# First-group weight sums read from a PSUM bank, and three weight blocks summed one group later

## The chip, the cores and the metric

The kernel runs on one core of a Trainium2 chip. The metric is the device time of one execution in microseconds (us); less is better. PE is the matrix engine, PEld its weight loads, DVE the vector engine, ACT the scalar engine, POOL is GpSimd, SP the engine whose queue issues all DMAs here. One group is 1024 of the 4096 tokens.

## What is computed

Cut to what matters, with `xn` the layer-normalised input (4096 tokens x 1024):

```python
g = sigmoid(xn @ gate_w.T + gate_b)          # the gate: first 1024 tokens feed the mean and y
h = silu(silu(xn @ w1.T) @ w3.T) @ w2.T      # experts' common network
out[top2 expert index] += gate * h           # so only rows 0..7 of the sum are not zero
x = x + s * silu(out)                        # s: recurrence over the gated, normalised input
```

Only rows 0 to 7 of the flattened output differ from the input; the kernel copies the rest. All products are float32. The mean over each batch row of the gated input needs the gate on the first 1024 tokens alone, so the gate product (kind `g`) exists for group 0 only; the two network products (kinds `u` for `w1` and `m` for `w3`) are made for all four groups.

## The kernel before, in words

**Products.** Each 1024 x 1024 x 1024 product is split once into 2 x 2 blocks of 512 and made with seven block products instead of eight (Strassen's scheme in Winograd's form). The seven are numbered 1 to 7. Each needs a left operand (a block of tokens, or one of the sums s1 to s4, lines 680 to 723) and a right operand (a block of a weight, or one of the sums T5, T6, T7, T4, made by `five`, `six`, `seven`, `four`, lines 557 to 584, for `w1` and `gate_w`, and by `take`, line 626, for `w3`). The change's title calls the sums of `six` and `four` T2 and T4. Each such block is a tile `b` of [128, 4, 512], so one sum is four instructions of 128x512.

**Inner level.** A block product that is not "plain" is split a second time in the same way (class `Half`, lines 762 to 846): seven small products of eight matmuls each, with four inner left sums (`left_sums`, 725) and four inner right sums (`fresh_sums`, 487, by `t_sum`, 471), all of them on POOL into tiles `q` of [128, 512]. A plain block product has eight small products and needs no inner sums. Plain are `u` 1 of group 0, `g` 1 and 2, and `m` 2 and 7 of group 0 (`PLAIN_M`).

**Results.** A small product lies in a PSUM tile X, Z or Y (X and Z have two buffers, Y one). Its result is taken out by ACT if it is the first of its output (`first`, 781), otherwise by DVE with an add `b<-X,b` ("drain" below). `whole` (879) adds finished blocks on DVE, and `done` starts the SILU on ACT.

**Later groups.** Groups 1 to 3 don't make the right operands again: `keep_block` and `keep_quarter` (475 to 485) write sums of group 0 to DRAM, `load_kept` and `load_kept_sum` (513, 519) read them. Three blocks have no inner sums from group 0, because they are plain there: `w1` block 1, whose four sums are made early in group 0 beside the product, by `kept_sums_1` (540), only to be kept; and `w3` blocks 2 and 7, whose sums are made in group 1 by `fresh_sums` with kind `m` and sb = 1 (lines 1097 to 1103), used there and kept for groups 2 and 3.

**Order.** The order of all instructions is written out by hand. A clock of "places" runs from 0 to 446 or so; each small product stands at one place (line 1151), other work is put at a place by `at(place, f)`, and a generator's `yield n` puts its rest n places later. Every engine executes its instructions in the resulting order, and so does SP its DMAs. `start[kind, group, i]` is the place of block product i: in group 0, `u` 2 at 16, 5 at 31, 6 at 45, 7 at 59, 4 at 73 and 3 at 87, with `g` three places after each and interleaved; then `m` 1, 5, 6, 2, 7, 4, 3 at 101, 108, 115, 122, 130, 138, 145; then seven places for each block product: `u` of group 1 from 152, `m` of group 1 from 201, with `m` 2 at 222 and `m` 7 at 229; `u` of group 2 from 250.

```python
def s_engine(kind, sb):
    return pool if kind == "u" and sb > 0 else dve
...
at(S(5) - 13, five)
at(S(6) - 16, six)
at(S(7) - 12, seven)
at(S(4) - 14, four)
```

So `five` (POOL) stands at places 18 and 21, `six` (DVE) at 29 and 32, `seven` (POOL) at 47 and 50, `four` (POOL) at 59 and 62, each first for `u` and then for `g`. s1 and s2 of `u` in group 0 are on DVE at 24 and 25, s4 at 75.

**Memory.** There are 20 tiles `b` and 18 tiles `q`, handed out first in, first out. `acc` is a PSUM bank that holds the scattered result from the middle of group 0's last stage on; before, it serves once for a row of statistics. `ps_acc` has a second tag, "rows", for the normalisation's rows of each group (`norm`, 352: DMA to a `q`, ACT copies it to the bank `bc`, DVE reads it from there).

Of the kernel before, what the change touches and what calls it, by code (L numbers as in the profile page):

```python
# [10 lines left out]
F32 = mybir.dt.float32  # L11
# [3 lines left out]
ALU = mybir.AluOpType  # L15
AX = mybir.AxisListType
P = 128
# [5 lines left out]
def kernel(  # L23
# [50 lines left out]
    H = 512  # L74
# [4 lines left out]
    class Pinned:  # L79
# [16 lines left out]
    pe, dve, act, pool, sync = (  # L96
        Pinned(e) for e in (nc.tensor, nc.vector, nc.scalar, nc.gpsimd, nc.sync)
    )
# [9 lines left out]
    ps_acc = ctx.enter_context(tc.tile_pool(name="ps_acc", bufs=1, space=bass.MemoryType.PSUM))  # L108
# [25 lines left out]
    def block(uses=1):  # L134
        return Held(blocks, uses)

    def quarter(uses=1):
        return Held(quarters, uses)
# [34 lines left out]
    acc = ps_acc.tile([P, H], F32, tag="acc", name="acc")  # L173
# [5 lines left out]
    def at(place, f, *args):  # L179

        seq[0] += 1
        heapq.heappush(todo, (place, seq[0], f, args))
# [17 lines left out]
    PLAIN_M = (2, 7)  # L200
# [7 lines left out]
    start = {}  # L208
# [244 lines left out]
    raw = {1: (0, 0), 2: (1, 0), 3: (1, 1)}  # L453
    weights = {"w1": w1, "gw": gw, "w3": w3}
    kept = {}
    op_t = {}
    op_ts = {}

    T_OF = ((1, 0, None), (3, None, 0), (3, 1, None), (2, None, 1))
    T_AT = (1, 2, 4, 6)  # L460
# [10 lines left out]
    def t_sum(o, t, s, j):  # L471
        p, q, e = T_OF[j]
        pool.tensor_tensor(o.tile, t[:, p], t[:, q] if q is not None else s[e].tile, ALU.subtract)

    def keep_quarter(name, i, j, o):
        d = dramp.tile([P, 2 * Q], F32, tag=f"{name}_{i}_{j}", name=f"{name}_{i}_{j}")
        sync.dma_start(d, o.tile)
        kept[name, i, j] = d
        o.drop()
# [4 lines left out]
        kept[name, i] = d  # L484
        t.drop()

    def fresh_sums(kind, sb, i, t, keep):

        name = {"u": "w1", "g": "gw", "m": "w3"}[kind]
        s = []  # L490
        for j in range(4):

            o = quarter(1 + (j < 2) + keep)
            t_sum(o, t, s, j)
            s.append(o)
            if j in (1, 3):
                s[(j - 1) // 2 if j == 1 else 1].drop()
            op_ts[kind, sb, i, j] = o
            if keep:
                at(start[kind, sb, i] + 2 * T_AT[j], keep_quarter, name, i, j, o)  # L500
            if j < 3:
                yield (T_AT[j + 1] - T_AT[j]) * 2
        t.drop()

    def sub(eng, out, p, q, n=4):

        for h in range(0, 4, 4 // n):
            eng.tensor_tensor(
                out[:, h : h + 4 // n], p[:, h : h + 4 // n], q[:, h : h + 4 // n], ALU.subtract
            )  # L510
            yield 0.5

    def load_kept(kind, sb, i, fresh):
        name = {"u": "w1", "m": "w3"}[kind]
        t = block(1 + fresh)
        sync.dma_start(t.tile, weights[name][raw[i]] if i in raw else kept[name, i])
        op_t[kind, sb, i] = t

# [5 lines left out]
    def first_weights(kind, name, before=()):  # L524

        keep = name == "w1"

        def S(i):
            return start[kind, 0, i]

        b = {}

        def load(key, KN, uses, *before):
            b[key] = load_w(name, KN, uses, *before)

        def one():

            op_t[kind, 0, 1] = b[1]

        def kept_sums_1():  # L540
            s = []
            for j in range(4):
                o = quarter(1 + (j < 2))
                t_sum(o, b[1], s, j)
                s.append(o)
                if j == 1:
                    s[0].drop()
                if j == 3:
                    s[1].drop()
                at(S(1) + 18 + 3 * j, keep_quarter, name, 1, j, o)  # L550
                yield 3
            b[1].drop()

        def two():
            op_t[kind, 0, 2] = b[2]

        def five():
            yield from sub(pool, b[5], b[5], b[1])
            b[1].drop()
            op_t[kind, 0, 5] = b[5]  # L560
            if keep:
                keep_block(name, 5, b[5])

        def six():
            yield from sub(dve, b[6], b[6], b[5])
            b[5].drop()
            op_t[kind, 0, 6] = b[6]
            if keep:
                keep_block(name, 6, b[6])

        def seven():

            yield from sub(pool, b[7], b[6], b[7])
            b[6].drop()
            op_t[kind, 0, 7] = b[7]
            if keep:
                keep_block(name, 7, b[7])

        def four():
            yield from sub(pool, b[4], b[4], b[6])  # L580
            b[6].drop()
            op_t[kind, 0, 4] = b[4]
            if keep:
                keep_block(name, 4, b[4])

        def three():
            op_t[kind, 0, 3] = b[3]

        off = 0 if kind == "u" else 1
        load(1, (0, 0), 2 + keep, before)  # L590
        one()
        if keep:
            at(S(1) + 8, kept_sums_1)
        at(-20 + off, lambda: load(2, (1, 0), 2))
        at(-19, two)
        at(-12 + off, lambda: load(5, (0, 1), 3 + keep))
        at(S(5) - 13, five)
        at(2 + off, lambda: load(6, (1, 1), 4 + keep))
        at(S(6) - 16, six)
        at(S(6) - 3 + off, lambda: load(7, (0, 0), 2 + keep))  # L600
        at(S(7) - 12, seven)
        at(S(6) + 8 + off, lambda: load(4, (1, 0), 2 + keep))
        at(S(4) - 14, four)
        at(S(3) - 14, lambda: load(3, (1, 1), 2))
        at(S(3) - 13, three)
        for i in order["u"][1:]:
            if kind == "g" and i in PLAIN_G:
                at(S(i) - 4, lambda i=i: op_t[kind, 0, i].drop())
                continue
            at(  # L610
                S(i) + 2 - (11 if i == 2 else 6),
                lambda i=i: fresh_sums(kind, 0, i, op_t[kind, 0, i], keep),
            )

    def first_w3():


        def S(i):
            return start["m", 0, i]

        b = {}

        def load(key, KN, uses):
            b[key] = load_w("w3", KN, uses)

        def take(i, p=None, q=None):

            if p is not None:
                for h in range(4):
                    dve.tensor_tensor(b[i][:, h], b[p][:, h], b[q][:, h], ALU.subtract)  # L630
                    yield 1
                (b[p] if i == q else b[q]).drop()
                keep_block("w3", i, b[i])
            op_t["m", 0, i] = b[i]

        for place, i, KN, uses in (
            (S(1) - 28, 1, (0, 0), 3),
            (S(1) - 27, 5, (0, 1), 4),
            (S(1) - 20, 6, (1, 1), 5),
            (S(2) - 14, 2, (1, 0), 2),  # L640
            (S(2) - 8, 7, (0, 0), 3),
            (S(7) - 10, 4, (1, 0), 3),
            (S(3) - 14, 3, (1, 1), 2),
        ):
            at(place, load, i, KN, uses)
        at(S(1) - 22, take, 1)
        at(S(1) - 20, take, 5, 5, 1)
        at(S(1) - 12, take, 6, 6, 5)
        at(S(2) - 8, take, 2)
        at(S(2) - 2, take, 7, 6, 7)  # L650
        at(S(7) - 3, take, 4, 4, 6)
        at(S(3) - 8, take, 3)
        for i in order["m"]:
            if i in PLAIN_M:
                at(S(i) - 4, lambda i=i: op_t["m", 0, i].drop())
                continue
            at(
                S(i) + 2 - {1: 16, 5: 12, 6: 10}.get(i, 6),
                lambda i=i: fresh_sums("m", 0, i, op_t["m", 0, i], True),
            )  # L660


# [426 lines left out]
    for kind, sb, i, plain in line:  # L1089
        h = Half(kind, sb, i, plain)  # L1090
        halves.append(h)
        S = start[kind, sb, i]
        n = 2 if sb == 0 and kind == "u" and i not in PLAIN_G else 1
        if kind != "g" and not plain:
            at(S + 2 - 8, left_sums, kind, sb, i, n)
        if kind != "g" and sb > 0:
            fresh = kind == "m" and sb == 1 and i in PLAIN_M
            at(S - (12 if fresh else 10), load_kept, kind, sb, i, fresh)
            if fresh:
                at(  # L1100
                    S - 5,
                    lambda i=i: fresh_sums("m", 1, i, op_t["m", 1, i], True),
                )
            for j in range(0 if fresh else 4):
                at(S + 2 * T_AT[j] - 9, load_kept_sum, kind, sb, i, j)

    for sb in range(NS):
        n = 2 if sb == 0 else 1
# [26 lines left out]
                )  # L1135
    at(start["u", 1, 1] + 25, recurrence)
    first_w3()

    w2_sb = {}

# [141 lines left out]
```

## Time and profile before

| what | value |
|---|---|
| median of 3 runs | 851.44 us (850.01 to 852.07) |
| the profiled execution | 850.65 us, of which the span from first to last instruction is 848.6 us |
| PE busy | 831.2 us, 98% |
| PEld busy | 701.9 us, 83% |
| DVE busy | 565.7 us, 67% |
| POOL busy | 496.6 us, 59% |
| ACT busy | 234.5 us, 28% |
| granted TensorE clock, mean | 0.997 |
| DMA | 189.71 MB, mean 224 GB/s |

The rows of the profile name a group of like instructions by line, engine, operation and tiles, out<-in. Since every engine call runs through one helper, all of them have line L89, and groups are told apart by tiles: `b` a block, `q` a quarter of one, X_u, Z_u, Y_u the PSUM tiles of kind `u`, `acc` and `bc` the other PSUM banks. In the timeline a row gives the start in us, the length, the engine, the operation, the tiles, how many instructions are merged in it, and in square brackets how long the engine had been idle and what ended that.

### The profile page before, as it was taken

The page shows a single profiled execution, that of the slowest core. Times are in us where ns is not written, and L with a number is a line of the kernel's source. Part 1 is how long each engine was busy: PE and PEld are TensorE (multiplying, and loading weights), DVE is VectorE, ACT ScalarE, POOL GpSimd, SP SyncE. Part 2 cuts the span into 40 slices and gives each one's busy share as a digit, 9 for nine tenths or more (in the row PEclk, how much of TensorE's full clock was granted, in tenths as well). Part 3 has the DMA queues.
Part 4 walks back from the last instruction along what each step waited for, and adds up shares of the span by engine and source line. Part 5 has one row for each costly group of instructions (what it writes and reads, how often), then busy time and mean ns, then how long its engine had stood idle before and what let it go on. Part 6 is the DMA issues. An engine that isn't in the chain of part 4 may idle for free.

```text
span 848.6 us, 11192 instructions
## 1 busy us (share of the span) xinstructions
PE 831.2 (98%) x4103; PEld 701.9 (83%) x4103; DVE 565.7 (67%) x889; ACT 234.5 (28%) x375; POOL 496.6 (59%) x375
## 2 busy tenths in 40 slices
PE   7999999989999999999999999999999999999997
PEld 6886888878888868888888778888888688888882
DVE  6989796988699425575897225775993246546642
ACT  0212213776121207343012226531122021220121
POOL 0389999995628764436866753753449444465400
PEclk9999999999999999999999999999999999999998
DMA  8953447631976877529976757659775455555600
GB/s 335 421 193 131 161 169 273 260 124 51 361 303 216 305 268 255 200 87 343 363 234 242 266 183 267 234 190 398 270 246 183 165 192 209 195 192 191 264 0 2
DMA packets 54013, 189.71 MB, mean 224 GB/s; under 512 B 6140, under 2 KB 9388, under 8 KB 42312
## 3 DMA queue, kind: packets, MB, share of 16 engines
q1 hardware_dynamic: 53960, 189.01, 60.2%
q8 instruction: 33, 0.54, 0.3%
q14 instruction: 20, 0.16, 0.1%
HBM read 165.86 MB, written 39.87 MB: 242 GB/s over the span
## 4 chain that ended last, share of the span: by engine, by line
PE 87%; DVE 7%; DMA 4%; SPq 1%; issue 1%; ACT 0%; DVEq 0%; ACTq 0%
PE X_u L89 21%; PE X_m L89 20%; PE Z_u L89 11%; PE Z_m L89 11%; DVE b L89 7%; PE Y_u L89 5%; PE X_g L89 5%; PE Y_m L89 4%; PE Z_g L89 3%; DMA b<-in_xT 3%; PE acc L89 2%; PE plT L89 2%; DMA b<-in_gw 1%; SPq L89 1%; PE Y_g L89 1%
## 5 line engine op out<-in xcount | busy, mean ns | idle before, releaser
L89 POOL TENSOR_TENSOR q<-b 128x512 f32<-128x512 f32 x144 | 202.8, 1421 | 230.6 <-DVE b L89 51.8
L89 ACT ACTIVATE b<-b 128x512 f32<-128x512 f32 (+1 forms) x152 | 105.0, 695 | 331.2 <-DVE b L89 322.1
L89 DVE TENSOR_TENSOR b<-b,b 128x512 f32<-128x512 f32 x176 | 181.8, 1052 | 3.3 <-POOL q L89 0.5
L89 POOL TENSOR_TENSOR q<-b,q 128x512 f32<-128x512 f32 x91 | 132.1, 1454 | 5.7 <-issue 3.3
L89 POOL TENSOR_TENSOR b<-b,b 128x512 f32<-128x512 f32 x72 | 94.5, 1336 | 40.5 <-PE X_u L89 34.4
L89 DVE TENSOR_TENSOR b<-X_u,b 128x512 f32<-128x512 f32 x87 | 59.9, 689 | 71.4 <-PE X_u L89 70.8
L89 PE MATMUL X_u<-q,q 128*128 128x256 f32 x432 | 103.1, 381 | 0.9 <-DVE b L89 0.9
L89 DVE TENSOR_TENSOR b<-X_m,b 128x512 f32<-128x512 f32 x84 | 57.2, 687 | 62.3 <-PE X_m L89 61.0
L89 PE MATMUL X_m<-q,q 128*128 128x256 f32 x416 | 98.3, 379 | 0.0
L89 PEld LDWEIGHTS X_u<-q,q 128*128 128x128 f32 x432 | 81.1, 190 | 16.1 <-issue 3.0
L89 POOL TENSOR_TENSOR q<-q,b 128x512 f32<-128x512 f32 x53 | 72.5, 1368 | 30.3 <-PE X_u L89 26.2
L89 PEld LDWEIGHTS X_m<-q,q 128*128 128x128 f32 x416 | 79.0, 190 | 10.8
L89 DVE TENSOR_TENSOR b<-b,bc 128x1024 f32<-128x1024 f32 (+1 forms) x62 | 72.8, 1178 | 3.6 <-ACT bc L89 2.5
L89 PE MATMUL X_m<-b,b 128*128 128x256 f32 x272 | 63.7, 380 | 0.9 <-DVE b L89 0.9
L89 PE MATMUL X_u<-b,b 128*128 128x256 f32 x248 | 58.8, 381 | 5.7 <-DVE b L89 5.5
L89 PEld LDWEIGHTS X_m<-b,b 128*128 128x128 f32 x272 | 51.3, 190 | 8.9 <-DVE b L89 1.9
L89 PEld LDWEIGHTS X_u<-b,b 128*128 128x128 f32 x248 | 46.8, 190 | 13.5 <-DVE b L89 6.7
L89 DVE TENSOR_TENSOR b<-Z_u,b 128x512 f32<-128x512 f32 x47 | 32.4, 689 | 28.6 <-PE Z_u L89 28.0
L89 PE MATMUL X_u<-b,q 128*128 128x256 f32 x216 | 51.3, 380 | 0.0
L89 PE MATMUL Y_u<-b,b 128*128 128x256 f32 x216 | 51.3, 380 | 0.0
L89 PE MATMUL Z_u<-q,b 128*128 128x256 f32 x216 | 51.3, 380 | 0.0
L89 DVE TENSOR_TENSOR b<-Z_m,b 128x512 f32<-128x512 f32 x48 | 32.8, 686 | 27.5 <-PE Z_m L89 26.1
(143 smaller groups left out, 1171.5 us busy)
## 6 DMA issues: line engine op xcount, KB each, us to landing
q<-w SPq DMA_DIRECT2D x160, 256.0 KB, 3.3
b<-in_w SPq DMA_DIRECT2D x35, 1024.0 KB, 7.4
b<-w_T SPq DMA_DIRECT2D x24, 1024.0 KB, 5.1
b<-in_xT SPq DMA_DIRECT2D x15, 1024.0 KB, 9.5
w<-q SPq DMA_DIRECT2D x56, 256.0 KB, 5.6
b<-in_x SPq DMA_DIRECT2D x12, 1024.0 KB, 7.3
w_T<-b SPq DMA_DIRECT2D x8, 1024.0 KB, 4.1
b<-in_gw SPq DMA_DIRECT2D x7, 1024.0 KB, 10.2
```

Source lines behind the costliest of these rows:

```text
L89: r = f(*args, **kwargs)
```

## The change

Five edits, of which the first two concern group 0's `u` and `g`:

1. `six` and `four` are made by a new function `with_bank`: ACT copies a quarter of the subtrahend into a PSUM bank (`acc` and a new tile of the tag "rows" by turns), and DVE subtracts with that bank as its second operand. The copy of quarter j+1 is issued ahead of the subtraction of quarter j. `six` was on DVE with both operands in SBUF, `four` on POOL. Places stay.
2. `kept_sums_1` goes. The same four sums of `w1` block 1 are made by `late_sums` from place 115 on (start of `m` 1, plus 14): it reads the block again from DRAM (1 MB), waits 5 places, and makes and keeps one sum every 2.5 places on POOL.
3. `w3` blocks 2 and 7: their inner sums are made by `late_sums` at places 156 and 170, in group 1's `u` stage, each with a load of 1 MB. Group 1's `m` 2 and 7 then take them from DRAM as in groups 2 and 3, so `fresh_sums` for group 1 goes.
4. `take` for `w3` blocks 7 and 4 moves from DVE to POOL, at the same places (120 and 127).
5. `take` for blocks 5 and 6, on DVE, moves two places later (from 81 to 83 and from 89 to 91).

```diff
+    def with_bank(out, p, q):
+        def copy(j):
+            spare[0] += 1
+            ps = acc if spare[0] % 2 else ps_acc.tile([P, H], F32, tag="rows", name="spare")
+            act.copy(ps, q[:, j])
+            return ps
+
+        ps = copy(0)
+        yield 0.5
+        for j in range(4):
+            ahead = copy(j + 1) if j < 3 else None
+            dve.tensor_tensor(out[:, j], p[:, j], ps, ALU.subtract)
+            ps = ahead
             yield 0.5
+    def late_sums(name, i):
+        t = block()
+        sync.dma_start(t.tile, weights[name][raw[i]] if i in raw else kept[name, i])
+        yield 5
+        s = []
+        for j in range(4):
+            o = quarter(1 + (j < 2))
+            t_sum(o, t, s, j)
+            s.append(o)
+            if j in (1, 3):
+                s[j // 2].drop()
+            yield 2.5
+            keep_quarter(name, i, j, o)
+        t.drop()
...
-            yield from sub(dve, b[6], b[6], b[5])
+            yield from with_bank(b[6], b[6], b[5])
...
-            yield from sub(pool, b[4], b[4], b[6])
+            yield from with_bank(b[4], b[4], b[6])
...
-        load(1, (0, 0), 2 + keep, before)
+        load(1, (0, 0), 2, before)
         one()
-        if keep:
-            at(S(1) + 8, kept_sums_1)
...
-                for h in range(4):
-                    dve.tensor_tensor(b[i][:, h], b[p][:, h], b[q][:, h], ALU.subtract)
-                    yield 1
+                yield from sub(pool if i in (7, 4) else dve, b[i], b[p], b[q], 4, 1)
...
-        at(S(1) - 20, take, 5, 5, 1)
-        at(S(1) - 12, take, 6, 6, 5)
+        at(S(1) - 18, take, 5, 5, 1)
+        at(S(1) - 10, take, 6, 6, 5)
...
-            fresh = kind == "m" and sb == 1 and i in PLAIN_M
-            at(S - (12 if fresh else 10), load_kept, kind, sb, i, fresh)
-            if fresh:
-                at(
-                    S - 5,
-                    lambda i=i: fresh_sums("m", 1, i, op_t["m", 1, i], True),
-                )
-            for j in range(0 if fresh else 4):
+            at(S - 10, load_kept, kind, sb, i)
+            for j in range(4):
                 at(S + 2 * T_AT[j] - 9, load_kept_sum, kind, sb, i, j)
...
+    at(start["m", 0, 1] + 14, late_sums, "w1", 1)
+    for n, i in enumerate(PLAIN_M):
+        at(start["u", 1, 1] + 4 + 14 * n, late_sums, "w3", i)
```

## The prediction

> **What bounds the kernel now.** I read the engines' shares first, then PE's waits, then the timeline around each wait.
>
> ```profile
> PE 831.2 (98%) x4103; PEld 701.9 (83%) x4103; DVE 565.7 (67%) x889; ACT 234.5 (28%) x375; POOL 496.6 (59%) x375
> PE X_u L89 <- DVE b L89: 6.4, 4, 2.4
> PE X_m L89 <- DVE b L89: 0.9, 1, 0.9
> ```
>
> PE sets the time. There are 446 small products of eight matmuls, one every 1.73 us where nothing stalls, 770 us in all; the rest is scatter, routing, start and tail, which the change leaves alone. So it can win only PE's waits for DVE, five waits of 7.3 us, and of those one of 1.5 us lies in the first 30 us, ahead of all that is changed. Now the others, each by two starts of PE; a start later than 1.73 us after the one before is lost time.
>
> ```profile
> 50.81 8.61 POOL L89 TENSOR_TENSOR b<-b,b 128x512 f32<-128x512 f32 x7
> 54.63 5.94 DVE L89 TENSOR_TENSOR b<-b,b 128x512 f32<-128x512 f32 x2
> 65.91 1.89 PE L89 MATMUL Z_g<-b,b 128*128 128x256 f32 x8
> 68.66 0.68 DVE L89 TENSOR_TENSOR b<-X_u,b 128x512 f32<-128x512 f32 x1
> 69.39 1.99 PE L89 MATMUL X_u<-b,b 128*128 128x256 f32 x8 [1.59 <-DVE b L89]
> ...
> 158.36 1.16 DVE L89 TENSOR_TENSOR b<-b,b 128x512 f32<-128x512 f32 x1
> 159.12 1.89 PE L89 MATMUL X_g<-q,q 128*128 128x256 f32 x8
> 161.12 0.68 DVE L89 TENSOR_TENSOR b<-X_u,b 128x512 f32<-128x512 f32 x1
> 161.94 1.97 PE L89 MATMUL X_u<-q,q 128*128 128x256 f32 x8 [0.94 <-DVE b L89]
> 170.65 1.89 PE L89 MATMUL Z_g<-q,b 128*128 128x256 f32 x8
> 174.17 0.68 DVE L89 TENSOR_TENSOR b<-X_u,b 128x512 f32<-128x512 f32 x1
> 174.91 1.99 PE L89 MATMUL X_u<-b,b 128*128 128x256 f32 x8 [2.36 <-DVE b L89]
> ```
>
> Each time PE waits for one drain `b<-X_u,b`, which takes 0.68 us itself but stands late in DVE's order behind `b<-b,b`. Stall A (place 31): 3.48 - 1.73 = 1.75. Stall B (places 81 and 87): 2.82 - 1.73 = 1.09, and 4.26 - 1.73 = 2.53, together 3.62. Stall C lies in group 1's `m` stage, at 430.10: 2.81 - 1.73 = 1.08, and 0.17 at 442.46, together 1.25. The sum, 6.6 us, is all there is to win. C has a control in the same profile: busy times by stretch, for group 1 (404 to 432) and the same places of group 2 (584 to 612); columns PE, PEld, DVE, ACT, POOL.
>
> ```profile
> 150.00:176.00 26.00, 22.70 (x104) 19.36 (x104) 25.13 (x32) 20.03 (x27) 26.00 (x17) 1.00 0.58 227
> 404.00:432.00 28.00, 27.08 (x126) 23.52 (x125) 25.16 (x28) 1.10 (x2) 24.39 (x18) 1.00 0.88 333
> 584.00:612.00 28.00, 28.00 (x131) 24.56 (x130) 24.64 (x30) 2.22 (x4) 10.72 (x8) 1.00 0.88 339
> ```
>
> Where POOL is busy 24 to 26 us, PE loses time; where it is busy 10.7, PE loses none, with as much DMA.
>
> **What the Trainium skill says.** "SBUF — State Buffer", Who interferes with whom: a DVE instruction with two SBUF inputs contends with a GpSimd instruction that reads SBUF, and the one that holds the shared pair blocks the other for the whole instruction; with one SBUF input it does not. The trace agrees: `b<-b,b` is 0.69 us alone and 1.16 to 1.75 beside POOL (mean 1052 ns of 176), in the first row above two take 5.94 us until POOL's run ends; the drains with a PSUM operand keep 0.68 beside the same POOL work, and POOL's 1.26 stretches to 1.72 only beside `b<-b,b`. "VectorE: DVE Perf Modes", the errata section: (N+151)/0.96, so 691 ns for 512 elements; the trace has 689 for `b<-X_u,b`. "ScalarE: Activation LUTs", What ACT_TABLE_LOAD costs: an activation without pointer operands is 186 + 0.833 N ns, 613 ns here; the trace has 590 ns for the row copy into a PSUM bank, `bc<-q`, the same operation as the new copies.
>
> **The change part by part.**
>
> Stall A. `kept_sums_1` is four POOL instructions. The first runs in a gap (POOL waits until 38.48 for the normalisation anyway), the other three stand between 39.7 and 48.4 in a run that has no gap until 59.42 and whose end is the seven `b<-b,b` above (`five`). Without them, at 8.61 / 7 = 1.23 us each, POOL's run ends 3.7 us earlier, at 55.7. DVE's first `b<-b,b` of s1 at 54.63 waits for just that, so s1, s2 and the drain behind them come 3.7 us earlier: X_u is free at 65.6 instead of 69.3, and PE wants it at 65.91 + 1.73 = 67.6. Margin 2 us, less up to 1.1 because POOL then also reaches its next sums earlier and contends with s2. Gain 1.75. Four stores of 256 KB leave SP's queue there; nobody waits for them.
>
> `six`: eight DVE `b<-b,b` between 69.26 and 82.8, 12.9 us in all, become eight of 0.69, 5.5 us, and POOL's sums beside them fall towards 1.26. PE has no wait there that this would remove (0 gained), but it covers the new wait: DVE now waits for ACT's copy, and behind the waiting instruction stand drains. Bound: 0 if the copies run ahead, 8 x (0.59 + about 0.1) = 5.5 us if each is waited for. Even then DVE has no more work than before. ACT's copies also stand ahead of its own drains of products 5, so ACT is tied to DVE's lateness; PE gives such a drain four slots, 6.9 us. Cost 0.
>
> `four`: POOL loses eight instructions between 119.5 and 136.5, 8 x about 1.4 = 11 us; DVE gets 8 x 0.69 = 5.5 us at places 59 to 64, 122.9 to 133 us. DVE's work there is six drains (4.1), one `whole` (1.0) and the 5.5, against 6 x 1.73 = 10.4 us of PE: 10.6, just full. The tight spot is the last drain of X_g of product 6 at place 60: PE wants the buffer at 128.03; DVE, free at 125.7, does two subtractions and then the drain, until 127.8. Margin 0.2 us if ACT's copies run ahead, which they can, since their source is ready long before. If not, up to 1 us is lost, and up to 0.6 at place 73 if the lateness isn't made up. Cost 0.4, bounds 0 and 1.6.
>
> Stall B. DVE's s4 stands at places 75 to 76.5: in the timeline four `b<-b,b` of 1.75, 1.16, 1.76 and 1.16, 5.8 us instead of 2.8, then a `whole` of 1.38. After the change POOL is 8 instructions ahead there. It can't use this beyond its next dependency: its left sums for product 3 need s4. So it runs dry some 10 us before s4 is made, s4 runs alone, and DVE leaves place 77 about 3.0 + 0.7 = 3.7 us earlier. That is more than the 1.09 us of B's first stall. After that POOL contends again, as before. The second stall needs the drain at 174.17 to end by about 171.3 (168.93 + 3.45, less the 1.09); it ends at 174.85 - 3.7 = 171.1, and one of the four `take` 5 instructions (1.15) falls behind it because of the shift by two places. But the other three come closer to it. I take 3.0 of 3.62 as won, with bounds 0 and 3.62.
>
> Stall C. The eight POOL sums of `w3` 2 and 7 leave 405 to 431. The stage becomes that of group 2, which has no stall. Gain 1.25. Instead the stage loads 8 x 256 KB more, which group 2 does as well. In group 1's `u` stage (286 to 343) POOL gets eight sums, 8 x 1.27 = 10 us, where it is busy 36 of 57 us and runs some 8 us or more ahead of PE; two loads of 1 MB and eight stores, with SP waiting for POOL at each store, where the DMA share is 0.74. Cost 0, since loads are issued nine places (15 us) ahead of use; at most 0.5.
>
> `take` 7 and 4, and the late sums of `w1`: POOL gets 8 + 4 instructions, 12 x 1.27 to 1.72 = 15 to 21 us, in 226 to 247, where it is idle for 19.7 us; DVE loses 8 x 0.69 = 5.5 us and more. The load of 1 MB at place 115 takes 2.5 us at 413 GB/s in a stretch with DMA share 1.0, and pushes group 1's blocks and rows behind it by as much. The first row copy (ACT, 238.3) waits for its landing already, and DVE's normalisation and drains behind it would be 2 us later; the nearest limit (last drain of `m` 6 before `m` 7 starts at 245.9) leaves about that. Cost 0.2, bounds 0 and 1.
>
> Sum: 1.75 + 3.0 + 1.25 - 0.4 - 0.2 = 5.4 us. From 850.65 that is 845.25. The median of the runs shown is 0.79 above the profiled one; I add half of that, **845.6**.
>
> **Rivals.** Something of 0.3%, 2.55 us, is about what a measurement of this kernel can tell from no change.
>
> First, B stays: POOL isn't dry at s4, or DVE's gated products (`SCALAR_TENSOR_TENSOR`, 1.75 and 1.18 beside POOL) and `take` 5 make up the same lateness. For it: POOL is 100% busy from 150 to 176. Against: the eight removed instructions stand directly ahead. Gain 2.4: 848.6.
>
> Second, the slow side: ACT and DVE go hand in hand at `four`. If each subtraction costs DVE its own 0.69, a copy of 0.59, two hand-overs and its share of the two 1.04 us statistics on ACT at places 60 and 61, about 1.6 us, DVE's work at places 59 to 64 is 4.1 + 1.0 + 12.8 = 17.9 against 10.4, PE waits about 7 us, and B stays. 850.65 - 3.0 + 7.0 + 0.4 = 855.0. It decides from about 1.4 us a subtraction. Against it: two banks, a copy issued ahead, and ACT busy only 10.3 of 36 us from 112 to 148.
>
> Third, no gain: the drains come earlier, but PE meets other late ones at the next places, so the stalls only move. About 851.0. Against it: between the stalls the drains follow their products by about 1.9 us, as early as they can.
>
> **How the numbers follow.** Forecast 0.67, own range 843.6 to 848.0 (all 6.6 won at no cost gives 844.0, or 844.4 with the half added; all costs at their bounds, 1.6 + 0.5 + 1.0, give 848). B stays 0.13, slow side 0.13, no gain 0.07. The range reaches over "B stays", up to 849.3. Faster by over 0.3% means under 848.9: the forecast and over half of the first rival, 0.74. Same 0.13, slower 0.13.
>
> **What would show it.** A: no PE wait at 69, s1's first instruction about 2 us or less instead of 5.3. B: POOL idle some us before s4, the four s4 instructions near 0.69, no PE wait of over 1 us between 155 and 175. C: group 1's `m` stage without a PE wait, POOL near 11 us in 28. `four`: copies `acc<-b` on ACT well ahead of DVE, DVE's `b<-b,acc` rows at 0.69 with no idle time before them. I'm wrong if those rows show DVE idle for ACT, if PE waits for DVE between 125 and 150, or if PE waits for POOL's `q` or for a DMA in groups 0 or 1.

## The result, and the profile after

| | median, us | lowest to highest | runs |
|---|---|---|---|
| before | 851.29 | 849.43 to 852.32 | 8 |
| after | 845.96 | 843.19 to 847.69 | 8 |

The ratio is 0.9936, with a 95% interval of 0.9916 to 0.9956: the change saves 3.7 to 7.2 us. The profiled execution of after took 847.3 us, with a span of 845.5 us and a mean granted clock of 0.993 (before: 850.65, 848.6 and 0.997).

The engines' shares of after, from the page:

```profile
PE 831.8 (98%) x4103; PEld 702.9 (83%) x4103; DVE 555.5 (66%) x889; ACT 243.5 (29%) x391; POOL 489.9 (58%) x375
L89 DVE TENSOR_TENSOR b<-b,b 128x512 f32<-128x512 f32 x160 | 155.4, 988 | 2.8
```

As many instructions on DVE and POOL as before, and 16 more on ACT: the copies. Before, DVE had 176 of `b<-b,b` at a mean of 1052 ns. Now PE's waits for DVE and POOL's `b`:

```profile
PE X_u L89 <- DVE b L89: 2.5, 2, 1.5
PE X_m L89 <- POOL b L89: 0.9, 1, 0.9
```

Of the 7.3 us of before, 3.4 are left. 1.5 of them is the wait ahead of all that was changed. One is what remains of stall B, and the last, for X_m, stands at a place where there was no wait before. I call it stall D. Start of PE by start of PE, with 1.73 us for a product that doesn't stall, the two traces differ in these places and no others by over 0.15 us:

| place | stall, us | before | after |
|---|---|---|---|
| 2 to 3 | head of the program, change only | | +2.1 |
| 31 | A | 1.75 | 0 |
| 81 | B, first | 1.09 | 0 |
| 87 | B, second | 2.53 | 1.15 |
| 130 | D, start of `m` 7 | 0 | 1.02 |
| 229, 236 | C | 1.08 and 0.17 | 0 |

The stalls give 4.46 us. The head takes 2.1 of it back in this execution, because the clock was granted at half for 6.83 us there (last section). Now the rows that answer to those shown of before. The first two fences are timelines of after, around stall A and around stall B.

```profile
46.27 8.65 POOL L89 TENSOR_TENSOR b<-b,b 128x512 f32<-128x512 f32 x7
...
56.68 1.28 DVE L89 TENSOR_TENSOR b<-b,b 128x512 f32<-128x512 f32 x2
...
67.69 0.68 DVE L89 TENSOR_TENSOR b<-X_u,b 128x512 f32<-128x512 f32 x1
67.95 1.89 PE L89 MATMUL Z_g<-b,b 128*128 128x256 f32 x8
69.68 1.89 PE L89 MATMUL X_u<-b,b 128*128 128x256 f32 x8
```

POOL's run of seven ends at 54.92 instead of 59.42. DVE's pair takes 1.28 us instead of 5.94, the drain ends at 68.37, and PE follows on after 1.73 us.

```profile
151.59 1.29 DVE L89 TENSOR_TENSOR b<-b,b 128x512 f32<-128x512 f32 x2
...
153.41 1.28 DVE L89 TENSOR_TENSOR b<-b,b 128x512 f32<-128x512 f32 x2
...
154.22 1.60 POOL L89 TENSOR_TENSOR q<-b 128x512 f32<-128x512 f32 x1 [9.30 <-issue]
...
155.21 1.17 DVE L89 TENSOR_TENSOR b<-b,b 128x512 f32<-128x512 f32 x1
...
161.03 1.89 PE L89 MATMUL X_u<-q,q 128*128 128x256 f32 x8
...
162.96 0.69 DVE L89 TENSOR_TENSOR b<-X_u,b 128x512 f32<-128x512 f32 x1 [1.03 <-PE X_u L89]
...
169.66 1.89 PE L89 MATMUL Z_g<-q,b 128*128 128x256 f32 x8
...
170.14 1.75 DVE L89 TENSOR_TENSOR b<-b,b 128x512 f32<-128x512 f32 x1
...
171.81 0.68 DVE L89 TENSOR_TENSOR b<-X_u,b 128x512 f32<-128x512 f32 x1
...
172.54 1.99 PE L89 MATMUL X_u<-b,b 128*128 128x256 f32 x8 [0.99 <-DVE b L89]
```

The four instructions of s4 are the second of the first row, the two of the row at 153.41, and the one at 155.21 (the first of all is a `whole`). POOL is idle for 9.30 us and starts again at 154.22, just after s4's second instruction is done (154.09). The profile names no releaser, but POOL's next sum reads the two quarters of s4 that these two instructions make. So the first three run at 0.68 us apiece, and the fourth takes 1.17 beside POOL: 3.2 us in place of the 5.8 of before. The first stall of B is gone: PE starts at 161.03 without a wait, and DVE is even idle for 1.03 us ahead of 162.96. Then a `b<-b,b` of 1.75, one of `take` 5, lies straight ahead of the drain that PE waits for at 172.54. Busy times by stretch in after (columns PE, PEld, DVE, ACT, POOL, clock, DMA share, GB/s):

```profile
150.00:176.00 26.00, 25.01 (x116) 21.69 (x115) 22.41 (x32) 21.50 (x31) 21.78 (x15) 1.00 0.51 189
222.00:250.00 28.00, 27.15 (x126) 23.62 (x125) 19.03 (x23) 4.31 (x6) 23.52 (x18) 1.00 1.02 408
404.00:432.00 28.00, 28.00 (x131) 24.56 (x130) 25.00 (x31) 2.22 (x4) 11.28 (x9) 1.00 0.89 341
```

Group 1's `m` stage (404 to 432) has become that of group 2: POOL at 11.28 instead of 24.39, PE at 28.00. The new loss is in the second row. The same stretch in before:

```profile
222.00:250.00 28.00, 28.00 (x131) 24.66 (x130) 23.06 (x32) 4.31 (x6) 7.12 (x6) 1.00 0.89 358
```

There POOL had 7.12 us of work instead of 23.52, and the DMA queues moved 358 GB/s instead of 408.

### The profile page after: what moved, and what is told of

The parts are those of the page before. It is cut to its first block, busy times and chain, and to the rows that moved or that the text cites. A ratio compares the mean times of both kernels' runs of the same rounds, so it can differ in the third digit from the quotient of the medians.

```text
span 845.5 us, 11244 instructions
## 1 busy us (share of the span) xinstructions
PE 831.8 (98%) x4103; PEld 702.9 (83%) x4103; DVE 555.5 (66%) x889; ACT 243.5 (29%) x391; POOL 489.9 (58%) x375
## 4 chain that ended last, share of the span: by engine, by line
PE 92%; DMA 3%; DVE 2%; POOL 1%; issue 1%; SPq 0%; ACT 0%; POOLq 0%; ACTq 0%; DVEq 0%
PE X_u L89 23%; PE X_m L89 20%; PE Z_u L89 12%; PE Z_m L89 11%; PE Y_u L89 6%; PE X_g L89 6%; PE Y_m L89 5%; PE Z_g L89 4%; PE acc L89 2%; PE plT L89 2%; DMA b<-in_w 2%; DMA w<-q 1%; DVE b L89 1%; POOL q L89 1%; PE Y_g L89 1%
## 5 line engine op out<-in xcount | busy, mean ns | idle before, releaser
L89 POOL TENSOR_TENSOR q<-b 128x512 f32<-128x512 f32 x144 | 198.4, 1391 | 232.3 <-DVE b L89 53.6
L89 DVE TENSOR_TENSOR b<-b,b 128x512 f32<-128x512 f32 x160 | 155.4, 988 | 2.8
L89 PE MATMUL X_u<-b,b 128*128 128x256 f32 x248 | 61.5, 394 | 2.8 <-DVE b L89 2.5
L89 PEld LDWEIGHTS X_u<-b,b 128*128 128x128 f32 x248 | 48.9, 198 | 11.0 <-DVE b L89 3.3
L89 PE MATMUL Z_u<-q,q 128*128 128x256 f32 x216 | 51.0, 379 | 0.0
```

The source lines that it names most:

```text
L89: r = f(*args, **kwargs)
```

## Experiments: each edit by itself

Each of these is before with one part of the change put in. What a stall is worth is read from PE's starts, as above, in the one profiled execution of each kernel; the medians are of several runs.

**Edit 1, the bank.** Before, and only:

```diff
-            yield from sub(dve, b[6], b[6], b[5])
+            yield from with_bank(b[6], b[6], b[5])
...
-            yield from sub(pool, b[4], b[4], b[6])
+            yield from with_bank(b[4], b[4], b[6])
```

> The kernel before with edit 1 alone: six and four read their subtrahend from PSUM banks on DVE. Theory (four's eight instructions leave POOL, which then runs dry before s4, so s4 runs alone): the 1.09 us at place 81 goes and the 2.53 us at place 87 falls by about half, since take 5 isn't shifted here; the stalls at 31 (1.75 us) and in group 1's m stage (1.25 us) stay. Gain 2 to 3 us. Rival (what helps at 81 and 87 is the shift of take 5 alone): both stalls stay, gain near zero or a loss, since DVE gets 2.6 us more work in all.

Measured: 846.09 us (845.27 to 846.75, 4 runs), ratio 0.9941 (0.9924 to 0.9958). By its median this edit alone is as fast as the whole change. Stall B loses 3.2 of its 3.62 us (0 and 0.41 are left), more than in after. Stall C stays. Stall A is 0.88 in this execution; the table near the end of the experiments comes back to it.

**Edit 2, the sums of `w1` later.** Before, with `kept_sums_1` and its call taken out, and:

```diff
+    at(start["m", 0, 1] + 14, late_sums, "w1", 1)
```

> The kernel before with edit 2 alone: the four sums of w1 block 1 leave the first products and are made late. Theory (POOL's run of sums ends some 3.7 us earlier, so DVE's s1 starts earlier): the PE stall of 1.75 us at place 31 is gone, those at places 81 and 87 (3.6 us together) and in group 1's m stage (1.25 us) stay; and if the new stall of 1.0 us at the start of m 7 comes from the extra load of 1 MB, it is here as well. Net gain 0.7 to 1.8 us. Rival (the stall at 31 goes because six reads a PSUM bank): it stays here, net gain zero or less. Rival for the new stall (POOL's take 7 and 4): no stall at m 7 here.

Measured: 849.32 us (846.46 to 850.93, 13 runs) against 850.56, ratio 0.9976 (0.9965 to 0.9988). Stall A is gone, B and C stay, and at `m` 7 there is a stall of 0.36 us. POOL's run of seven ends at 54.58 (54.92 in after), and DVE's pair takes 1.28 us. PE is late in this execution, though: its first `g` product starts at 18.96 instead of 16.59.

**Edit 3, the sums of `w3` in group 1's `u` stage.**

```diff
-            fresh = kind == "m" and sb == 1 and i in PLAIN_M
+            fresh = False
...
+    for n, i in enumerate(PLAIN_M):
+        at(start["u", 1, 1] + 4 + 14 * n, late_sums, "w3", i)
```

> The kernel before with edit 3 alone: the sums of w3 blocks 2 and 7 are made in group 1's u stage. Theory: the stalls of 1.08 and 0.17 us in group 1's m stage go, nothing else changes, no new stall from 286 to 345 us. Gain 1.25 us. Rival (the stall there comes from DVE's own load and the DMAs, not from POOL's sums): it stays, and eight more loads of 256 KB make it no better.

Measured: 848.0 us (846.98 to 850.23, 5 runs), ratio 0.9964 (0.9945 to 0.9983). Stall C loses 1.08 + 0.18, nothing comes up in the `u` stage. But stall A is gone here too, without edit 2, and the first stall of B is longer by 0.53 us. Neither can be the work of edit 3, whose first instruction stands at place 156. The last of the experiments come back to stall A.

**Edits 4 and 5, `take`.**

```diff
-                    dve.tensor_tensor(b[i][:, h], b[p][:, h], b[q][:, h], ALU.subtract)
+                    (pool if i in (7, 4) else dve).tensor_tensor(b[i][:, h], b[p][:, h], b[q][:, h], ALU.subtract)
...
-        at(S(1) - 20, take, 5, 5, 1)
-        at(S(1) - 12, take, 6, 6, 5)
+        at(S(1) - 18, take, 5, 5, 1)
+        at(S(1) - 10, take, 6, 6, 5)
```

> The kernel before with edits 4 and 5 alone: take 7 and 4 on POOL, take 5 and 6 two places later. Theory: the stall at place 31 and the one in group 1 stay; of the 3.6 us at places 81 and 87 at most 1 us goes, since one take 5 instruction of about 1.15 us falls behind the late drain; no stall at m 7, because the extra load of 1 MB is missing here. Gain 0 to 1 us. Rival for m 7 (POOL's take 7 and 4 hold PE up, as the profile's releaser says): the stall of about 1 us at m 7 is here.

Measured: 849.7 us (847.85 to 851.39, 13 runs), ratio 0.9991 (0.998 to 1.0002), no change that can be told. No stall at `m` 7. The stall at place 87 falls from 2.53 to 2.07 us. In this execution and in that of edit 2 PE also loses 1.7 us at places 88 and 89, to the clock (last section).

## Experiments: what makes the bank worth its copies

**Both sums on DVE, from SBUF.** After, without the copies:

```diff
-            yield from with_bank(b[6], b[6], b[5])
+            yield from sub(dve, b[6], b[6], b[5])
...
-            yield from with_bank(b[4], b[4], b[6])
+            yield from sub(dve, b[4], b[4], b[6])
```

> The kernel after, with six and four on DVE from SBUF operands, without the bank and the copies: it tells the move off POOL from the bank. Theory (the bank matters, since b<-b,b shares a port with POOL and costs 1.05 to 1.75 us beside it): four's eight subtractions take 8 to 14 us instead of 5.5 at places 59 to 64, where DVE is full already, so PE waits 2 to 6 us for drains between 122 and 150; slower than after by 2 to 6 us. Rival (it is enough that POOL loses the eight instructions): within 1 us of after, no PE wait there.

Measured: 848.99 us (847.71 to 849.92, 18 runs) against 850.74, ratio 0.9978 (0.9969 to 0.9988). Against after, PE loses 2.96 us at place 62, 0.26 at 68 and 0.93 at 73. The timeline of this kernel at place 62:

```profile
126.60 2.82 DVE L89 TENSOR_TENSOR b<-b,b 128x512 f32<-128x512 f32 x2
...
129.35 0.68 DVE L89 TENSOR_TENSOR b<-X_g,b 128x512 f32<-128x512 f32 x1
...
130.08 1.99 PE L89 MATMUL X_g<-b,b 128*128 128x256 f32 x8 [2.79 <-DVE b L89]
```

And of after at the same place:

```profile
126.01 0.67 DVE L89 TENSOR_TENSOR b<-b,acc 128x512 f32<-128x512 f32 x1
126.61 0.67 DVE L89 TENSOR_TENSOR b<-b,spare 128x512 f32<-128x512 f32 x1
...
127.20 0.68 DVE L89 TENSOR_TENSOR b<-X_g,b 128x512 f32<-128x512 f32 x1
...
128.22 1.89 PE L89 MATMUL X_g<-b,b 128*128 128x256 f32 x8
```

The same two subtractions ahead of the same drain take 2.82 us with both inputs in SBUF beside POOL, and 1.27 with one of them in PSUM. At places 31, 81 and 87 this kernel has PE's starts of after, so what is won of stall B is won without the bank, by what POOL no longer has to do. The bank keeps the moved sums from costing PE 4.15 us at places 62 to 73. So it is the bank that makes it pay to have `four` on DVE: without it the kernel keeps only 1.75 us of its gain (850.74 - 848.99) instead of 5.33.

**One bank, no copy ahead.** After, with the ACT copy and the subtraction hand in hand, which is the mechanism of my slow rival:

```diff
-        ps = copy(0)
         yield 0.5
         for j in range(4):
-            ahead = copy(j + 1) if j < 3 else None
-            dve.tensor_tensor(out[:, j], p[:, j], ps, ALU.subtract)
-            ps = ahead
+            act.copy(acc, q[:, j])
+            dve.tensor_tensor(out[:, j], p[:, j], acc, ALU.subtract)
```

> The kernel after, with a single bank (acc) and no copy issued ahead, so that each subtraction waits for its own copy: the slow rival's hand in hand. If it is as that rival priced it, a subtraction costs DVE about 1.4 us (0.69 + 0.59 + two hand-overs) and PE waits 4 to 7 us for drains between 122 and 150. If DVE finds other work between, as its drains stand between the subtractions, PE loses 1 to 3 us. If ACT's copies hide in any case, nothing changes.

Measured: 846.11 us (844.16 to 847.92, 6 runs), ratio 0.994 (0.9922 to 0.9959). PE loses 0.45 us at place 62. The timeline of this kernel there:

```profile
124.52 0.59 ACT L89 COPY acc<-b 128x512 f32<-128x512 f32 x1 [17.99 <-DVE b L89]
...
125.14 0.69 DVE L89 TENSOR_TENSOR b<-b,acc 128x512 f32<-128x512 f32 x1 [0.66 <-ACT acc L89]
...
126.49 1.99 PE L89 MATMUL X_g<-b,b 128*128 128x256 f32 x8 [0.29 <-DVE b L89]
```

The copy takes 0.59 us and DVE waits 0.66 for it, as the rival said, so a subtraction that waits costs about 1.3 us. But the waits don't add up to the 7 us on PE that it foretold. Of the eight subtractions of `four` only four wait, 2.5 us together, for the 0.45 us of PE. Of those of `six` seven wait, 6.0 us together, and PE loses nothing. Which slack takes up the rest, these runs don't show. The second bank saves less than can be told by the medians.

## Experiments: the new stall D, and what is left of B

**The late sums of `w1` later still.** After, and:

```diff
-    at(start["m", 0, 1] + 14, late_sums, "w1", 1)
+    at(start["m", 0, 1] + 26, late_sums, "w1", 1)
```

> The kernel after, with the late sums of w1 block 1 started 12 places (some 21 us) later, so that their 1 MB isn't read among group 1's first loads. Theory (the 1.0 us that PE loses at the start of m 7 comes from DVE waiting for the row copy, whose DMA stands behind that load): it is gone, DVE's wait before its first normalisation falls from 3.1 us to 1 or less; gain about 1 us. Rival (POOL's take 7 and 4 hold PE, as the profile's releaser says): the stall stays.

Measured: 844.68 us (842.81 to 845.23, 4 runs), ratio 0.9917 (0.9892 to 0.9943). Stall D is gone (1.02 less at place 130), nothing else moves.

**`take` 7 and 4 on DVE again.** After, without edit 4:

```diff
-                yield from sub(pool if i in (7, 4) else dve, b[i], b[p], b[q], 4, 1)
+                yield from sub(dve, b[i], b[p], b[q], 4, 1)
```

> After with edit 4 alone undone: take 7 and 4 on DVE. The wait at the start of m 7 stays at about 1.0 us if it is the 1 MB load's doing, as the later load showed. If POOL's additional work also holds it, it falls below 0.7. Otherwise the same as after: 846, at most 0.5 to either side.

Measured: 844.28 us (842.64 to 846.68, 6 runs), ratio 0.9918 (0.9898 to 0.9937). Stall D falls from 1.02 to 0.20. So either step by itself nearly frees the place: D needs both. Three timelines show how. First after:

```profile
226.54 2.84 SPq L89 DMA_DIRECT2D q<-flat  x2
...
238.57 0.59 ACT L89 COPY bc<-q 128x512 f32<-128x512 f32 x1 [9.73 <-POOL b L89]
...
239.19 1.22 DVE L89 TENSOR_TENSOR b<-b,bc 128x1024 f32<-128x1024 f32 x1 [3.10 <-ACT bc L89]
...
241.05 1.69 DVE L89 TENSOR_TENSOR b<-b,b 128x512 f32<-128x512 f32 x1
...
241.82 1.89 PE L89 MATMUL X_m<-b,b 128*128 128x256 f32 x8
...
243.79 0.68 DVE L89 TENSOR_TENSOR b<-X_m,b 128x512 f32<-128x512 f32 x1
244.57 5.42 PE L89 MATMUL X_m<-b,b 128*128 128x256 f32 x24 [0.85 <-POOL b L89]
```

Then the kernel with the sums of `w1` at 127:

```profile
224.03 2.85 SPq L89 DMA_DIRECT2D q<-flat  x2
...
236.07 0.59 ACT L89 COPY bc<-q 128x512 f32<-128x512 f32 x1 [7.17 <-DMA q<-flat]
```

And the one with `take` 7 and 4 on DVE:

```profile
238.70 1.22 DVE L89 TENSOR_TENSOR b<-b,bc 128x1024 f32<-128x1024 f32 x1 [1.25 <-ACT bc L89]
...
240.56 0.69 DVE L89 TENSOR_TENSOR b<-b,b 128x512 f32<-128x512 f32 x1
...
242.90 0.68 DVE L89 TENSOR_TENSOR b<-X_m,b 128x512 f32<-128x512 f32 x1
```

The 1 MB load stands ahead of the row loads `q<-flat` in SP's queue, and SP issues them 2.51 us later with it (226.54 against 224.03). ACT's copy of the row and DVE's normalisation are later by the same 2.50 (238.57 against 236.07). The profile of after names POOL's `b` as what ended ACT's wait; it was done at 238.50, and the trace has the row's landing at 238.49. The late row by itself costs 0.20 to 0.36 us of PE (the kernel with `take` 7 and 4 on DVE, and edit 2 alone). The rest, 0.8 us, is the sum of three things. The `b<-b,b` of 1.69 us between the normalisation and the last drain of `m` 6, with POOL's `take` beside it, is 1.0 longer than the 0.69 that it takes when POOL is idle. The normalisation starts 0.4 later against PE than in the last kernel shown. And DVE is spared one subtraction of `take`, 0.6. For PE's wait, too, the profile names POOL's `b`. By time it was the drain, which ended at 243.79 + 0.68 = 244.47, 0.10 ahead of PE.

**`take` 5 and 6 at their old places.** After, without edit 5:

```diff
-        at(S(1) - 18, take, 5, 5, 1)
-        at(S(1) - 10, take, 6, 6, 5)
+        at(S(1) - 20, take, 5, 5, 1)
+        at(S(1) - 12, take, 6, 6, 5)
```

> The kernel after without edit 5: take 5 and 6 back at places 81 and 89. Theory (the shift brings three of the four take 5 instructions closer to the last drain of u 4, as edit 1 alone left only 0.4 us of the stall at place 87 and the whole change 1.15): the stall at place 87 falls to 0.5 us or less; gain 0.7 us. Rival (what the whole change leaves at place 87 comes from the w1 or w3 edits): it stays at about 1.15 us.

Measured: 845.06 us (844.12 to 845.22, 4 runs), ratio 0.9926 (0.9903 to 0.9948). The stall at place 87 falls from 1.15 to 0.40. The timeline of this kernel:

```profile
160.39 0.80 DVE L89 TENSOR_TENSOR b<-b,b 128x512 f32<-128x512 f32 x1
...
161.50 0.69 DVE L89 TENSOR_TENSOR b<-X_u,b 128x512 f32<-128x512 f32 x1 [0.32 <-PE X_u L89]
...
162.87 1.75 DVE L89 TENSOR_TENSOR b<-b,b 128x512 f32<-128x512 f32 x1
...
169.61 0.68 DVE L89 TENSOR_TENSOR b<-X_u,b 128x512 f32<-128x512 f32 x1
...
170.34 1.99 PE L89 MATMUL X_u<-b,b 128*128 128x256 f32 x8 [0.24 <-DVE b L89]
```

At the old places the first instruction of `take` 5 uses DVE's idle time at 160 (in after DVE idles 1.03 us there instead, ahead of 162.96), and the slow one of 1.75 comes seven microseconds before the drain. Edit 5 moves one instruction behind the drain, as I had it, but it also pushes the other three out of idle time and closer to it. It costs 0.75 us net in this kernel, while in before edits 4 and 5 together took 0.45 off the same stall.

## Experiments: what is needed of the change

Three combinations. The first is after without edit 5 and with the sums of `w1` at place 127, the second is the same without edit 4 as well, the third has edits 1 and 3 alone.

```diff
-        at(S(1) - 18, take, 5, 5, 1)
-        at(S(1) - 10, take, 6, 6, 5)
+        at(S(1) - 20, take, 5, 5, 1)
+        at(S(1) - 12, take, 6, 6, 5)
...
-    at(start["m", 0, 1] + 14, late_sums, "w1", 1)
+    at(start["m", 0, 1] + 26, late_sums, "w1", 1)
```

> After, with edit 5 undone (take 5 and 6 back at places 81 and 89) and the late sums of w1 moved from place 115 to 127. Each of the two alone had taken 0.75 and 1.02 us of PE waits off. If they are independent, PE's wait for X_u before place 88 falls to about 0.4 us, the one at the start of m 7 is gone, and the time is 1.8 us below after: 844.2 us (843 to 845). If the two share a cause, or the median of the runs is set by the clock that is granted rather than by these waits, it isn't below the better one alone, 844.7 to 845.1.

> The same with edit 4 undone as well: take 7 and 4 on DVE as before. If moving them to POOL has no value, the same waits and the same time within 0.3 us, 844.2. If DVE needs the relief, its eight b<-b,b of 0.7 us return between 209 and 245 us and PE shows a wait of 0.2 us or more at a drain there; at most 1 us slower.

> Edits 1 and 3 alone: w1's four sums are made early on POOL as before, nothing is at place 115. If edit 2 is worth its stall A only in executions whose head ran at full clock, PE waits up to 1.75 us at place 31 where it did, less where a slow-clock window of about 2.1 us lies in the head; the median is then 0.5 to 1.5 us above the kernel without edits 4 and 5, about 845. If edit 2 is worth the whole of stall A always, 1.75 us above, 846. If it is worth nothing, equal to it, 844.2.

| kernel | median, us | lowest to highest (6 runs each) | ratio (95% interval) |
|---|---|---|---|
| edits 1, 2 at place 127, 3, 4 | 843.32 | 841.76 to 844.43 | 0.9906 (0.9889 to 0.9924) |
| edits 1, 2 at place 127, 3 | 844.75 | 844.26 to 845.88 | 0.9928 (0.9912 to 0.9944) |
| edits 1, 3 | 844.11 | 843.64 to 845.28 | 0.9922 (0.9906 to 0.9938) |

The first has both gains in full: 0.76 less at place 87 and 1.02 less at place 130 than after. They are independent, and this is the fastest kernel of the study. Its interval overlaps that of after, so that it beats after is likely, not certain.

The second has a new stall of 0.92 us at places 140 and 142 (258 to 263 us), later than where I had looked for one. The first, with `take` 4 on POOL, has none there, nor has the third, with `take` 4 on DVE but without the late sums of `w1`. So this stall takes both, `take` 4 on DVE and the late sums at place 127, and edit 4 is of use where edit 2 is late. That DVE's sums with two SBUF inputs and POOL's late sums contend in one stretch is my reading of it; no run takes that apart. No other run shows a use of edit 4.

The third does without edit 2, so that stall A should be back. In its profile it isn't, although POOL's run is as late as before:

```profile
50.56 9.98 POOL L89 TENSOR_TENSOR b<-b,b 128x512 f32<-128x512 f32 x7
...
55.25 2.48 DVE L89 TENSOR_TENSOR b<-b,b 128x512 f32<-128x512 f32 x2
```

In before these two rows are 50.81 with 8.61 and 54.63 with 5.94. There DVE's pair waits until POOL's last of seven is done; here the engines take turns, DVE's two are done after 2.48 us, and POOL's seven take 1.37 longer. With it I can say what stall A depends on. Five profiled kernels have the early sums of `w1`:

| kernel | first `g` product starts at | DVE's pair: start, length | stall A |
|---|---|---|---|
| before | 16.59 | 54.63, 5.94 | 1.75 |
| edits 4, 5 | 16.86 | 54.79, 5.36 | 1.16 |
| edit 1 | 17.82 | 55.75, 5.08 | 0.88 |
| edit 3 | 18.64 | 56.57, 3.75 | 0 |
| edits 1, 3 | 17.32 | 55.25, 2.48 | 0 |

In the first four the pair ends between 60.15 and 60.83, just after POOL's run, which ended between 59.00 and 59.67 however late PE was. PE's own time depends on its first products. If these are slow by 2 us, the drain is there when PE arrives. In the fifth the pair wasn't held up.

## Why the prediction was right, and where it was not

The forecast was 845.6 against 845.96, with the mechanism named for each stall. Its terms beside what the two profiles show:

| term | predicted, us | measured, us |
|---|---|---|
| stall A | -1.75 | -1.75 |
| stall B | -3.0 | -2.47 |
| stall C | -1.25 | -1.26 |
| `four` | +0.4 | 0 |
| `take`, late `w1` | +0.2 | +1.02 |
| `six`, `w3` sums in the `u` stage | 0 | 0 |
| sum | -5.4 | -4.46 |

The predicted 5.4 and the medians' 5.33 lie nearer to each other than these terms do. That is luck within the interval of 3.7 to 7.2. Part of the medians' 5.33 is probably the clock: in the 60 runs of before that were made beside the experiments and the eight of after, the spans with a mean granted clock of 0.995 average 848.34 (20 runs) and 844.15 (2 runs), those with 0.993 average 850.17 (19) and 845.45 (2). That is 4.2 and 4.7 us, an estimate on few runs of after, but near the 4.46 of the stalls. After had a mean clock of 0.999 in three of its eight runs, before in none of the 60.

**A.** The chain was right: POOL's run ended 4.5 us earlier (I had 3.7), the pair ran alone, and the margin at the drain was there. What I didn't see is that the 1.75 us is the size of the stall in the one execution that was profiled, the one with the fastest first products of the five above. In the other four executions it is 1.16, 0.88, 0 and 0. In after the first products were slow as well, so its own profile doesn't show that edit 2 is needed. But two profiles with edit 2 have first `g` products as early as before's 16.59 (one bank: 16.45; edits 1, 2 at place 127 and 3: 16.53); both have edit 1 as well. In both the drain is done at 66.2 to 66.3, PE goes on at 67.5 to 67.6 without a stall, and the margin of 1.3 us lies within the forecast one. Edit 2 is thus worth up to 1.75 us in an execution. Alone, it was 1.24 us faster by the medians, of which spans at one clock (0.995, 7 runs against 20) leave 0.45; beside edits 1 and 3, with and without it (843.32 with edit 4, 844.75 without, against 844.11), it is worth nothing that these runs can tell.

**B.** "So it runs dry some 10 us before s4 is made" held: POOL was idle for 9.30 us until s4's second quarter was there. It then caught the fourth instruction of s4, 1.17 us instead of 0.69, so s4 wins 2.6 us and not the 3.0 of the forecast. (The `whole` stands ahead of s4, not behind it as the forecast reads it; that changes no sum.) Even so the first stall is gone, and with edit 1 alone 3.2 us of B are won, more than the 3.0 that I took. The step that failed is "one of the four `take` 5 instructions (1.15) falls behind it" with "But the other three come closer to it". I had the two effects and set them equal. Undoing the shift shows the second to be larger, by 0.75 us. The Trainium skill's "SBUF — State Buffer", Who interferes with whom, tells only of the contention of single instructions; here the cost came from idle time of DVE that the shift left unused (1.03 us ahead of 162.96).

**C.** Right in place and size, with edit 3 alone as the proof, and the control of group 2 was the right way to see it.

**`four`.** I had 0.2 us of margin and took 0.4 as the cost; place 62 shows none. The two subtractions and the drain took 126.01 to 127.88, as worked out. The bound of 5.5 us for `six` and the slow rival's 1.6 us a subtraction both rest on DVE's waits for ACT adding up on PE's path. With one bank they were there (eleven waits of 8.5 us together) and cost PE 0.45 us in all. With two banks the copies ran ahead at `four`, but not everywhere at `six`: DVE waited 0.59, 0.49 and 1.55 us for ACT there, and PE lost nothing by it. The slow side is right about the waits and refuted in what they cost PE.

**`take` and late `w1`.** The place (last drain of `m` 6 before `m` 7) and the cause (the 1 MB load pushes the row load by 2.5 us) were foretold, and 2.51 was measured. The term was mis-sized: 0.2 for 1.02, just past its bound of 1. I weighed the load's 2 us against the limit's 2 us, and weighed POOL's `take` as a relief for DVE only. But its instructions contend with a `b<-b,b` in the same stretch, 1.69 instead of 0.69, and the two lateness terms add up behind a margin that either alone nearly fits into.

**The rivals.** "B stays" is refuted by edit 1 alone. "No gain", that the stalls only move, is right in kind at one place (D), for 1.02 of 5.5 us.

## What to carry to other kernels

Where DVE and POOL share a stretch, look for the sums with two SBUF inputs ahead of a drain that the matrix engine waits for, and let an idle ACT copy one input to PSUM: here that edit, which also took eight sums off POOL, gave as much by itself as all five. Before shifting work to "later" or to a free engine, add up everything that becomes late at the next drain, loads in the issue queue and contention together, since margins of 2 us were used up by two harmless-looking edits at once. A stall read from one profiled execution is one sample: look at where the engine that waits and the engine that releases each get their timing from, and whether another execution could shift one against the other.

## What I had not expected of the hardware

**Half clock in short windows.** The first sixteen matmuls `X_u<-b,b`, first in before, then in after:

```profile
12.29 3.72 PE L89 MATMUL X_u<-b,b 128*128 128x256 f32 x16 [1.50 <-DVE b L89]
...
12.35 6.56 PE L89 MATMUL X_u<-b,b 128*128 128x256 f32 x16 [1.50 <-DVE b L89]
```

The clock records of after show TensorE granted half its clock from 11.3 to 18.1 us. Of the fourteen profiled kernels, three have no such window in the head (before, one bank, and edits 1 to 3 with `w1` at 127), five have one of 3.41 us (edit 1 alone: 5.41 us for the sixteen matmuls), six one of 6.83. So the profile of before, on which I sized stall A, is of the rarer kind among these. Two kernels (edit 2, and edits 4 and 5) have another 3.41 us in the middle, at places 88 and 89, where PE lost 1.64 and 1.69 us. All fourteen have such windows at the end. This accounts for part of the spread of one kernel's runs: after's spans are 845.4 to 845.9 us at a mean clock of 0.993 or 0.994, and 841.4 to 841.9 at 0.999. What sets the windows, no run here shows.

**A blocked pair that waits for a whole run, or doesn't.** The same two DVE instructions beside the same seven of POOL waited for the end of the run in four profiles and took turns in one (5.94 against 2.48 us). The Trainium skill's "SBUF — State Buffer", Who interferes with whom, says that whichever issues first gets the shared pair and blocks the other for the whole instruction; the first four agree only if POOL's next instruction gets the pair ahead of the waiting DVE each time. What decides that, no run here shows.
